# A selective-scan stage on one Trainium2 core: dt's product leaves PSUM by Relu, the second half's x projection is done in one go from DRAM, the gate of y comes a slot later, and dt's sum is on GpSimd

## The chip, the cores and the metric

The kernel runs on one core of one Trainium2 chip. The metric is device time in microseconds of one execution. Engines are called PE (TensorE), DVE (VectorE), ACT (ScalarE), POOL (GpSimd) and SP (SyncE, which here only issues transfers). All data are fp32; a few matmul operands are read in the fp32r format. The core has on-chip memory of 128 partitions (SBUF), and PSUM with eight banks of 128 x 512 fp32, into which PE writes.

## The reference

Eight layers run one after the other on an activation of 2 x 1024 x 1024, each with a residual and a layer norm: attention, grouped feed-forward, convolution with block attention, a binary-weight product, a selective scan, an int4 product, attention, and a product with routed low-rank terms. Only the selective scan (the reference's `_L2_attn_ref`) is touched:

```python
proj = hidden_states @ in_proj_w                      # 1024 -> 2 x 2048
x, z = split(proj)
xc = silu(conv_b + causal 4-tap convolution of x)     # per channel, along time
ssm_p = einsum('bdl,ed->ble', xc, x_proj_w)           # 2048 -> 64 + 16 + 16
dt_r, Bm, Cm = rmsnorm of the three parts of ssm_p
dt = softplus(dt_r @ dt_proj_w.T + dt_bias)           # 2048 channels
A = -exp(A_log)                                       # 2048 x 16
h = exp(dt * A) * h + dt * B * x                      # step by step in time, 16 states per channel
y = (sum over the states of h * C + D * xc) * silu(z)
out = y @ out_proj_w.T
```

The kernel writes softplus(p) as max(p, 0) + ln(1 + e) + (e - ((1 + e) - 1)) with e = exp(-|p|); the last bracket gives back what is lost when 1 + e is rounded.

## The kernel before, in words

The program treats the two batch elements one after the other, and everything in this section happens twice. In the scan layer a batch element has 1024 time steps, taken as two halves of 512 (`u` = 0, 1), and 2048 channels, taken as 16 chunks of 128 (`c`).

**What comes before the scans.** `l2_in` (L999) computes the first half: for each chunk a product of eight matmuls into a PSUM bank, a copy with the convolution's first tap on ACT (`l2_x`), three taps on DVE (`l2_taps`, L985), Silu on ACT, a write of the result to DRAM (`xcd`, L991), and the x projection (`l2_px`, L997), which accumulates over the chunks in one PSUM bank. `l2_norm` and `l2_spread` turn that bank into dt_r, B and C.

**The slots.** The scan is a loop over slots `k`, with its order written out by hand (a manual schedule: each engine receives its instructions in the order of the text). A chunk of one half takes 8 slots, 128 slots make a half, 256 both. A slot handles 2 x 128 rows, each row a (state, channel) pair with 512 time steps:

- SP loads `h` (L1117, 128 rows x 2 x 512): dt times x of the slot's channels, read from DRAM (`dxd`) so that 16 partitions get the same row. It is issued six slots ahead; there are nine buffers.
- POOL multiplies `h` by B, two slots ahead (`times_b`, L1123).
- PE spreads dt over the states (`decay`, L1130), and ACT takes the exponent in place in PSUM (L1132), one slot ahead, twice a slot.
- DVE runs two scans (L1137), and multiplies the slot before by C (`times_c`, L1148).
- PE sums the states into the bank `py` of the chunk (`states`, L1159), every second slot.

**Work on a chunk's edge.** Work for later slots is put down with `at(slot, f)`; it runs in the middle of its slot, behind the first scan, the first decay and its exponent, and ahead of the second scan. For each chunk `l2_dt` (L1055) starts 16 slots before the chunk's own scans: the product p on PE (L1060) in the first slot, and then one step per slot, in this order:

```python
for n, f in enumerate((act1, act2, pool1, sum1, parts, low)):
    at(k + 1 + n, f)
at(k + 8, load)
```

`act1` takes Abs of p and Exp (L1071, L1072), `act2` 1 + e and Ln (L1075, L1076), `pool1` three operations on POOL (L1079 to L1081), `sum1` adds max(p, 0) on DVE straight out of PSUM (L1084), `parts` copies dt to `hi` on ACT (L1087) and multiplies it by x on POOL (L1088, x comes in as `xi`, whose load is issued at slot k + 3), and writes the product to `dxd` (L1090), `low` makes the low part on POOL (L1093) and writes `hi` and `lo` to DRAM (L1095); `load` reads them back (L1100). The tiles `e`, `one`, `lg`, `hi` and `lo` have one buffer each.

At the end of a chunk `y_out` (L1175) multiplies the bank `py` by silu(z) on DVE (L1177) and writes it to DRAM. Its operand `zs` (one buffer) is loaded by `y_in` at slot 4 of each eight, and `y_out` is put down five slots later, in the same slot as the last `states` of that chunk.

**Work beside the scans.** PE has other matmuls to do in the meantime; they stand in a list, `todo`, and each slot takes the next 17 of every 8 slots in the first half, 14 of 8 in the second: the gates of the first half (128 matmuls), the x of the second half (`ins(1)`, 128 matmuls, each chunk followed by taps, Silu and x projection through `at`), the gates of the second half (128), and from slot 140 on the out product of the first half (`outs(0)`). The loads of the weights stand in a queue of their own, `ahead`, in order, each with the number of calls by which it goes ahead.

**Buffers.** All PSUM tiles share one pool of eight banks. `self.w()` gives one of eight buffers of 128 x 1024, of which two hold dt's weights through the layer. SP takes its transfers in the order of the text, and waits at one that isn't ready.

Of the kernel before, what the change touches and what calls it, by code (L numbers as in the profile page):

```python
# [8 lines left out]
F = mybir.dt.float32  # L9
I = mybir.dt.int32  # L10
R = mybir.dt.float32r
AF = mybir.ActivationFunctionType
ALU = mybir.AluOpType
# [4 lines left out]
P = 128  # L18
# [9 lines left out]
class Net:  # L28
# [892 lines left out]
    def l2_attn(self, b):  # L921
# [4 lines left out]
        with (  # L926
# [4 lines left out]
            cw = self.param(lp, "l2_convw", [P, NCH, 4])  # L931
            cb = self.param(lp, "l2_convb", [P, NCH])
            dpar = self.param(lp, "l2_D", [P, NCH])
            A = self.param(lp, "l2_Alog", [P, NCH * N])
            nc.scalar.activation(A, A, AF.Exp)
            nc.vector.tensor_scalar(A, A, -1.0, None, ALU.mult)
# [34 lines left out]
            def at(k, f, *args):  # L971
                late.setdefault(k, []).append((f, args))
# [21 lines left out]
            def l2_px(u, c, acc):  # L994
                if c == 0:
                    px[u] = self.ps()
                nc.tensor.matmul(  # L997
                    px[u][:NF, :], wx[:, c * NF : (c + 1) * NF], acc, start=c == 0, stop=c == NCH - 1
                )  # L999
# [57 lines left out]
            def l2_dt(u, c, k):  # L1057

                p = self.ps()
                nc.tensor.matmul(  # L1060
                    p, wd[c // 8][: NF + 1, (c % 8) * P : (c % 8 + 1) * P], norms[u][0], start=True, stop=True
                )
                xs[u, c] = xc = tmp("xi")
                at(k + 3, nc.sync.dma_start, xc, xcd[u][c][:])
                e, one, lg = tmp("e", 1), tmp("one", 1), tmp("lg", 1)
                dt, dtx = lg, e
                hi = tp.tile([P, HALF], R, tag="hi", bufs=1, name=self.nm("hi"))
                lo = tp.tile([P, HALF], R, tag="lo", bufs=1, name=self.nm("lo"))

                def act1():  # L1070
                    nc.scalar.activation(e, p, AF.Abs)  # L1071
                    nc.scalar.activation(e, e, AF.Exp, scale=-1.0)  # L1072

                def act2():
                    nc.scalar.activation(one, e, AF.Identity, bias=self.one)  # L1075
                    nc.scalar.activation(lg, one, AF.Ln)  # L1076

                def pool1():
                    nc.gpsimd.tensor_scalar(one, one, 1.0, None, ALU.subtract)  # L1079
                    nc.gpsimd.tensor_tensor(e, e, one, ALU.subtract)  # L1080
                    nc.gpsimd.tensor_tensor(lg, lg, e, ALU.add)  # L1081

                def sum1():
                    nc.vector.scalar_tensor_tensor(dt, p, 0.0, lg, ALU.max, ALU.add)  # L1084

                def parts():
                    nc.scalar.copy(hi, dt)  # L1087
                    nc.gpsimd.tensor_tensor(dtx, dt, xc, ALU.mult)  # L1088
                    for j in range(4):
                        nc.sync.dma_start(dxd[u][c][:, j, :], dtx[32 * j : 32 * j + 32, :])  # L1090

                def low():
                    nc.gpsimd.tensor_tensor(lo, dt, hi.bitcast(F), ALU.subtract)  # L1093
                    for s, t in ((0, hi), (1, lo)):
                        nc.sync.dma_start(hld[u][c][:, s, :], t.bitcast(F))  # L1095

                def load():
                    t = qp.tile([P, 2, HALF], F, tag="hl", bufs=2, name=self.nm("hl"))
                    for s in range(2):
                        nc.sync.dma_start(  # L1100
                            t[64 * s : 64 * s + 64], hld[u][c][:, s, :].rearrange("(a r) t -> r a t", a=2)
                        )
                    hl[u, c] = t
# [4 lines that stand above are left out]
# [72 lines left out]
            def ins(u):  # L1180

                def one(u, c):
                    u0 = u * HALF
                    w = {}

                    def load():
                        w["w"] = self.w(i["l2_in"][c])

                    def call(k, now):
                        if k == 0:  # L1190
                            w["p"] = self.ps()
                        p = w["p"]
                        nc.tensor.matmul(  # L1193
                            p, w["w"][:, k * P : (k + 1) * P], self.xcols(k, u0, HALF), start=k == 0, stop=k == KD - 1
                        )
                        if k == KD - 1:
                            def x():
                                w["x"] = l2_x(u, c, p)
                            at(now + 1, x)
                            at(now + 2, lambda: l2_taps(c, p, w["x"]))  # L1200

                            def s():
                                w["s"] = l2_silu(u, c, p)
                                self.table()
                            at(now + 3, s)
                            at(now + 5, lambda: l2_px(u, c, w["s"]))
                            if c == NCH - 1:
                                at(now + 6, lambda: at(now + 8, l2_spread, u, l2_norm(u)))
                    return load, [(call, k) for k in range(KD)]
                return [one(u, c) for c in range(NCH)]  # L1210

            def gates(u):

# [70 lines left out]
            with self.tc.manual_schedule():  # L1284

                todo, ahead = [], []

                def take(units, lead):
                    for n, (load, calls) in enumerate(units):
                        ahead.append((len(todo) - lead, load))  # L1290
                        todo.extend(calls)

                take(gates(0), 20)
                take(ins(1), 20)
                take(gates(1), 20)
                taken = 0
                at(-BEFORE, lambda: at(4 - BEFORE, l2_spread, 0, l2_norm(0)))
                for k in range(-BEFORE, 2 * SL + 6):
                    if -16 <= k < 2 * SL - 16 and k % 8 == 0:
                        l2_dt((k + 16) // SL, (k + 16) % SL // 8, k)  # L1300
                    if k == SL + 12:
                        take(outs(0), 8)
                    if k == -1 or k == SL:
                        l2_cr(max(k, 0) // SL)
                    n = 3 if k < -1 else 2 + (k % 8 == 0) if k < SL else 2 - (k % 4 == 3)
                    batch = []
                    for _ in range(n):
                        while ahead and ahead[0][0] <= taken:
                            ahead.pop(0)[1]()
                        if taken < len(todo):  # L1310
                            batch.append(todo[taken])
                            taken += 1

                    def pe(last=False):
                        while batch and (last or len(batch) > n - 1):
                            f, *args = batch.pop(0)
                            if f:
                                f(*args, k)

                    live = 0 <= k < 2 * SL  # L1320
                    if 0 <= k + 6 < 2 * SL:
                        rows(k + 6)
                    if 0 <= k + 2 < 2 * SL:
                        times_b(k + 2)
                    if 0 <= k - 1 < 2 * SL:
                        keep(k - 1)
                    pe()
                    for m in range(2):
                        if live:
                            scan(k, m)  # L1330
                        if 0 <= k + 1 < 2 * SL:
                            decay(k + 1, m)
                        if m:
                            break
                        if k % 2 == 1 and 0 <= k - 2 < 2 * SL:
                            states(k - 2)
                        for f, args in late.pop(k, []):
                            f(*args)
                        pe(True)
                    if 0 <= k - 1 < 2 * SL:  # L1340
                        times_c(k - 1)
                    if live and k % 8 == 4:
                        v = y_in(k)
                        at(k + 5, lambda k=k, v=v: y_out(k, v))
                    if live and k % 8 == 0:
                        skip(k // SL, k % SL // 8)
                while late:
                    for f, args in late.pop(min(late)):
                        f(*args)
# [439 lines left out]
```

## Time and profile before

| | |
|---|---|
| Time, median of 3 runs | 5673.8 us (5659.03 to 5676.83) |
| Profiled execution, its own time | 5686.25 us |
| Its span | 5684.5 us |
| Busy share of the span: PE, DVE, POOL, ACT | 88%, 57%, 36%, 33% |
| Mean granted TensorE clock | 0.934 |
| Slots 0 to 255 of the first batch element | 1174.7 to about 2236 us |
| Slots 0 to 255 of the second | 4014.7 to about 5060 us |
| One scan (L1137), `times_c` (L1148), on DVE | 1.21 to 1.27, 1.195 us |
| `times_b` (L1123), on POOL | 2.37 us |
| One exponent (L1132), on ACT | 0.66 us |
| dt's sum (L1084) and y's gate (L1177), on DVE | 0.67 and 0.69 us |
| POOL with a scalar (L1079), POOL with two tensors (L1080, L1081, L1088, L1093), 128 x 512 | 1.49, 1.27 us |

The busy share is a mean over eight layers with different limits; the scans take about 2107 of 5684 us. "Idle before" an instruction is the time its engine stood still ahead of it, put down to what ended it. A wait of SP holds back all transfers behind it. The share of the DMA engines counts the time in which they have packets in work, and the rate in GB/s what they moved.

### The profile page before, as it was taken

To read this page: it belongs to the slowest core of one execution; us is meant where nothing else is said; L and a number is where in the kernel's file an instruction comes from. 1 tells how busy PE (TensorE), PEld (TensorE's weight loads), DVE (VectorE), ACT (ScalarE), POOL (GpSimd) and SP (SyncE) were. 2 spreads that over 40 slices of the span, in tenths; PEclk is the share of its full clock that TensorE was granted. 3 is DMA by queue.
4 is the path that set the end of the run, shared out by engine and by line. 5 is a ranking of instruction groups with operands and counts; after the bars stand their busy time and mean duration, and the time that the engine had idled before them with its cause. 6 is when DMAs were issued, how large, how long until landed. Compare 5 with 4: busy or idle time off the path is not lost.

```text
span 5684.5 us, 50188 instructions
## 1 busy us (share of the span) xinstructions
PE 5023.3 (88%) x16840; PEld 2396.8 (42%) x16840; DVE 3258.3 (57%) x4474; ACT 1858.8 (33%) x3795; POOL 2033.7 (36%) x1193
## 2 busy tenths in 40 slices
PE   9879979998888887998989799899988887889989
PEld 4346646433333222454444376464333332234533
DVE  3553245269889897214345412452798999962243
ACT  2320232266656442001013311323666564420010
POOL 1031120077678774100010211200776787741000
PEclk8889988999999998999988899889999999989999
DMA  2135301298789997201110333012987899961100
GB/s 90 41 126 178 100 32 43 97 242 236 214 224 270 253 261 209 81 30 41 48 67 30 115 123 99 30 42 100 251 231 217 232 267 261 270 196 61 60 8 30
DMA packets 295094, 782.85 MB, mean 138 GB/s; under 512 B 40976, under 2 KB 58000, under 8 KB 294836
## 3 DMA queue, kind: packets, MB, share of 16 engines
q1 hardware_dynamic: 288564, 758.66, 46.8%
q0 software_dynamic: 6272, 20.98, 1.1%
q8 instruction: 135, 2.21, 0.2%
q14 instruction: 123, 1.01, 0.1%
HBM read 640.81 MB, written 136.58 MB: 137 GB/s over the span
## 4 chain that ended last, share of the span: by engine, by line
PE 43%; DVE 13%; DMA 8%; ACT 3%; issue 3%; POOL 2%; SPq 0%; DVEq 0%; POOLq 0%; ACTq 0%
PE ps L104 21%; DVE h L1137 5%; PE ps L1436 4%; PE ps L579 3%; PE ps L1226 3%; DVE h L1148 3%; PE ps L1159 2%; DMA xi<-xcd 2%; DMA h<-dxd 2%; PE ps L120 2%; POOL h L1123 1%; ACT ps L1132 1%; PE ps L1130 1%; DMA w<-yd 1%; DVE x L165 1%
## 5 line engine op out<-in xcount | busy, mean ns | idle before, releaser
L1123 POOL TENSOR_TENSOR h<-h,br 128x1024 f32<-128x1024 f32 x512 | 1199.2, 2366 | 67.6 <-DMA h<-dxd 38.8
L1132 ACT ACTIVATE ps<-ps,l_Alog 128x512 f32<-128x512 f32 x1024 | 666.8, 659 | 844.9 <-PE ps L1130 818.7
L1130 PE MATMUL ps<-hl,rep 128*128 128x512 f32 x1024 | 706.1, 701 | 137.4 <-DVE h L1137 106.3
L1137 DVE TENSOR_TENSOR_SCAN h<-ps,h 128x512 f32<-128x512 f32 x512 | 608.7, 1211 | 68.6 <-ACT ps L1132 65.8
L1137 DVE TENSOR_TENSOR_SCAN h<-ps,hst,h 128x512 f32<-128x512 f32 x512 | 635.4, 1269 | 19.8 <-POOL h L1123 18.5
L1148 DVE TENSOR_TENSOR h<-h,ps 128x1024 f32<-128x1024 f32 x512 | 611.4, 1195 | 0.0
L1159 PE MATMUL ps<-h,sel 128*32 128x512 f32 x2048 | 462.1, 656 | 131.0 <-DVE h L1148 128.9
L104 PE MATMUL ps<-w,xT 128*128 128x512 f32 (+1 forms) x1280 | 515.6, 560 | 0.0
L1226 PE MATMUL ps<-xT,w 128*128 128x512 f32 x1024 | 515.2, 607 | 0.1
L1130 PEld LDWEIGHTS ps<-hl,rep 128*128 128x128 f32 x1024 | 201.2, 199 | 563.6 <-DVE h L1137 325.6
L131 DVE TENSOR_TENSOR x<-x,ps 128x512 f32<-128x512 f32 x192 | 129.3, 683 | 519.2 <-PE ps L104 369.6
L1422 POOL TENSOR_TENSOR x<-x,row 128x1024 f32<-128x1024 f32 x48 | 113.2, 2361 | 876.3 <-PE ps L120 876.3
L104 PE MATMUL ps<-xT,w 128*128 128x512 f32 x960 | 425.1, 599 | 0.2 <-DMA w<-l_wqkv 0.2
L104 PEld LDWEIGHTS ps<-w,xT 128*128 128x128 f32 x1280 | 246.5, 194 | 253.5 <-issue 246.6
L120 PE MATMUL ps<-ident,x 128*128 128x128 f32 x1024 | 166.0, 318 | 180.7 <-DVE x L165 153.4
L1079 POOL TENSOR_SCALAR one<-one 128x512 f32<-128x512 f32 x64 | 95.5, 1493 | 575.1 <-ACT lg L1076 544.2
L1226 PEld LDWEIGHTS ps<-xT,w 128*128 128x128 f32 x1024 | 188.6, 191 | 223.0 <-issue 202.2
L104 PEld LDWEIGHTS ps<-xT,w 128*128 128x128 f32 x960 | 183.9, 192 | 233.3 <-issue 232.5
L1193 PE MATMUL ps<-xT,w 128*128 128x512 f32 x512 | 275.9, 626 | 2.8 <-DVE h L1137 2.8
L1265 PE MATMUL ps<-w,w 128*128 128x512 f32 x512 | 275.0, 619 | 2.2 <-DVE h L1137 2.2
L156 ACT ACTIVATE rs<-mv 128x1 f32<-128x1 f32 (+2 forms) x94 | 19.1, 203 | 780.5 <-DVE mv L150 780.2
L985 DVE SCALAR_TENSOR_TENSOR ps<-xp,l_convw,ps 128x512 f32<-128x512 f32 x192 | 144.5, 753 | 199.0 <-ACT ps L980 194.4
(262 smaller groups left out, 7234.0 us busy)
## 6 DMA issues: line engine op xcount, KB each, us to landing
h<-dxd SPq DMA_DIRECT2D x512, 512.0 KB
w<-l_in SPq DMA_DIRECT2D x128, 512.0 KB
w<-l_out SPq DMA_DIRECT2D x96, 512.0 KB
hl<-hld SPq DMA_DIRECT2D x128, 256.0 KB
w<-l_conv SPq DMA_DIRECT2D x54, 512.0 KB
w<-cvd SPq DMA_DIRECT2D x36, 512.0 KB
w<-l_fw SPq DMA_DIRECT2D x32, 512.0 KB
xcd<-xo SPq DMA_DIRECT2D x64, 256.0 KB
```

What stands on the lines that cost most here:

```text
L104: self.nc.tensor.matmul(out, lhsT, rhs, start=j == 0, stop=j == n - 1)
L120: nc.tensor.transpose(p[:, j * P : (j + 1) * P], self.x[:, tt, k * P : (k + 1) * P], self.ident)
L1123: nc.gpsimd.tensor_tensor(hs[k], hs[k], norms[of(k)[0]][1].unsqueeze(1).to_broadcast([P, 2, HALF]), ALU.mult)
L1130: nc.tensor.matmul(dA[k, m], rep[:, 4 * m + q, :], hl[u, c][:, jj, :].bitcast(R), start=True, stop=True)
L1132: nc.scalar.activation(dA[k, m], dA[k, m], AF.Exp, scale=A[:, g : g + 1])
L1137: nc.vector.tensor_tensor_scan(hs[k][:, m, :], dA.pop((k, m)), hs[k][:, m, :], hst[:, g : g + 1] if u else 0.0, ALU.mult, ALU.add)
L1148: nc.vector.tensor_tensor(hs[k], hs[k], norms[of(k)[0]][3].unsqueeze(1).to_broadcast([P, 2, HALF]), ALU.mult)
L1159: nc.tensor.matmul(py[u, c][32 * j : 32 * j + 32, :], self.sel[:, q, :], hs[k - 1 + j // 2][:, j % 2, :], start=False, stop=q == 3,)
L1193: nc.tensor.matmul(p, w["w"][:, k * P : (k + 1) * P], self.xcols(k, u0, HALF), start=k == 0, stop=k == KD - 1)
L1226: nc.tensor.matmul(p, w["w"][:, k * P : (k + 1) * P], self.xcols(k, u * HALF, HALF), start=k == 0, stop=k == KD - 1)
L1265: nc.tensor.matmul(p, y[:, cc, t * P : (t + 1) * P], wt[:, cc * HALF : (cc + 1) * HALF], start=c2 == 0 and cc == 0, stop=last,)
L1436: nc.tensor.matmul(acc[tt], y[:, cc * HALF + tt * P : cc * HALF + (tt + 1) * P], w[:, cc * HALF : (cc + 1) * HALF], start=c == 0, stop=c = ...
```

## The change

- **dt's product leaves PSUM by Relu.** `act1` first writes max(p, 0) to `hi` on ACT. `sum1` is no longer a DVE operation on PSUM, but an addition on POOL of two tiles in SBUF. The bank of p is free after `act1` (slot k + 1), where it was held to `sum1` (slot k + 4).
- **(1 + e) - 1** is a third operation of `act2` on ACT, with a tile of -1 as its bias; it was POOL's operation with a scalar.
- **x projection of the second half.** `ins(1)` no longer calls `l2_px`, `l2_norm` and `l2_spread`. New units, `xproj(1)`, stand in the list of matmuls behind the first two units of the gates of the second half: eight units, each of two transfers of 256 KB from `xcd` into one `w` buffer, and two calls. Their loads go four calls ahead (those of the gates twenty), and the loads of the later gates stand behind them in `ahead`.
- **The gate of y** is put down six slots after `y_in`, where it was five.

```diff
+            neg = lp.tile([P, 1], F, name=self.nm("neg"))
+            nc.gpsimd.memset(neg, -1.0)
...
                 def act1():
+                    nc.scalar.activation(hi.bitcast(F), p, AF.Relu)
                     nc.scalar.activation(e, p, AF.Abs)
                     nc.scalar.activation(e, e, AF.Exp, scale=-1.0)
 
                 def act2():
                     nc.scalar.activation(one, e, AF.Identity, bias=self.one)
                     nc.scalar.activation(lg, one, AF.Ln)
+                    nc.scalar.activation(one, one, AF.Identity, bias=neg)
 
                 def pool1():
-                    nc.gpsimd.tensor_scalar(one, one, 1.0, None, ALU.subtract)
                     nc.gpsimd.tensor_tensor(e, e, one, ALU.subtract)
                     nc.gpsimd.tensor_tensor(lg, lg, e, ALU.add)
 
                 def sum1():
-                    nc.vector.scalar_tensor_tensor(dt, p, 0.0, lg, ALU.max, ALU.add)
+                    nc.gpsimd.tensor_tensor(dt, lg, hi.bitcast(F), ALU.add)
...
-                            at(now + 5, lambda: l2_px(u, c, w["s"]))
-                            if c == NCH - 1:
-                                at(now + 6, lambda: at(now + 8, l2_spread, u, l2_norm(u)))
...
+            def xproj(u):
+
+                def one(c2):
+                    w = {}
+
+                    def load():
+                        w["x"] = self.w()
+                        for n in range(2):
+                            nc.sync.dma_start(w["x"][:, n * HALF : (n + 1) * HALF], xcd[u][2 * c2 + n][:])
+
+                    def call(n, now):
+                        l2_px(u, 2 * c2 + n, w["x"][:, n * HALF : (n + 1) * HALF])
+                        if 2 * c2 + n == NCH - 1:
+                            at(now + 1, lambda: at(now + 3, l2_spread, u, l2_norm(u)))
+                    return load, [(call, n) for n in range(2)]
+                return [one(c2) for c2 in range(NCH // 2)]
...
-                take(gates(1), 20)
+                z1 = gates(1)
+                take(z1[:2], 20)
+                take(xproj(1), 4)
+                take(z1[2:], 20)
...
-                        at(k + 5, lambda k=k, v=v: y_out(k, v))
+                        at(k + 6, lambda k=k, v=v: y_out(k, v))
```

## The prediction, made before the result was known

> **What bounds the kernel now.** The change touches the scan layer alone, so I read stages first: the busy time by stretch (first batch element; slots 0 to 32, 32 to 88, 88 to 112, 112 to 160, 160 to 256). Columns: PE, PE weight loads, DVE, ACT, POOL busy, PE clock, DMA share, GB/s.
>
> ```profile
> 1174.70:1296.00 121.30, 113.33 (x341) 43.89 (x340) 111.78 (x103) 80.98 (x150) 97.65 (x52) 1.00 0.99 256
> 1296.00:1554.90 258.90, 218.43 (x630) 79.37 (x630) 231.42 (x228) 169.43 (x313) 183.95 (x96) 0.94 0.84 224
> 1554.90:1668.60 113.70, 90.86 (x272) 34.83 (x271) 99.52 (x103) 60.84 (x119) 72.81 (x39) 0.91 0.80 213
> 1668.60:1844.00 175.40, 158.44 (x484) 59.24 (x484) 173.10 (x157) 109.91 (x183) 151.99 (x80) 0.98 1.01 267
> 1844.00:2236.00 392.00, 306.76 (x870) 105.47 (x869) 359.95 (x330) 154.34 (x252) 281.09 (x143) 0.90 0.95 249
> ```
>
> DVE is busiest everywhere, but its idle differs: 9.5, 27.5, 14.2, 2.3 and 32.0 us. The transfers differ too: the first, fourth and fifth stretches move 249 to 267 GB/s, near the fastest stretch I found (275), and only the second and third have room. The waits of DVE say what each idle is. Slots 32 to 88:
>
> ```profile
> DVE zs L1177 <- PE ps L1159: 13.4, 7, 3.4
> DVE h L1137 <- ACT ps L1132: 11.6, 9, 3.0
> ```
>
> Half of it is y's gate standing in front of the state sums of its own slot, half a scan whose exponent is late. Slots 160 to 256:
>
> ```profile
> DVE lg L1084 <- POOL lg L1081: 14.5, 6, 4.5
> DVE h L1137 <- POOL h L1123: 12.5, 5, 4.2
> DVE zs L1177 <- PE ps L1159: 4.5, 6, 0.8
> ```
>
> Here POOL is late, and POOL's own waits in that stretch give the cause, x's transfer:
>
> ```profile
> POOL e L1088 <- DMA xi<-xcd: 47.1, 8, 8.3
> POOL h L1123 <- DMA h<-dxd: 13.7, 13, 2.4
> ```
>
> Last, the timeline of SP and ACT around a chunk's edge in that stretch, for the new use of `hi`:
>
> ```profile
> 2080.36 0.53 SPq L1095 DMA_DIRECT2D hld<-hi  x1
> ...
> 2082.66 0.59 ACT L1071 ACTIVATE e<-ps 128x512 f32<-128x512 f32 x1
> ...
> 2086.79 0.59 SPq L1100 DMA_DIRECT2D hl<-hld  x1
> ```
>
> SP issues L1100 when `hi` has landed in DRAM: 4.1 us after the next chunk's Abs began.
>
> **What the Trainium skill says.** "ScalarE: Activation LUTs", section on table sets: relu, copy, identity and abs are in every set, so Relu and Identity bring no table load; the trace agrees for Abs and Identity between Exp and Ln (a load would show as 1.28 us). "SBUF — State Buffer", section on its two sides: GpSimd and a DVE operation with two SBUF inputs exclude each other for a whole instruction. The scans and the product with C take one operand from PSUM, and keep their 1.21 and 1.195 us under a busy POOL; the norm's tiny DVE operations do not (L1027 took 2.40 us, a POOL product 2.37). So POOL's new addition doesn't slow the scans. "Perfetto Trace Analysis", optimization strategy: a gap that repeats can mean that no PSUM buffer was free. The trace agrees: PE's decays wait for DVE's scans, 106 us before the matmul and 326 before its weights.
>
> **The change, part by part.** Per batch element, against the profiled execution; 32 chunks, 0.67 us per dt sum.
>
> *DVE loses the sum:* 32 x 0.67 = 21.4 us of work, worth something only where DVE sets the pace. *POOL* trades 1.49 for 1.27 us. *ACT* gains a Relu (0.59, as Abs from PSUM) and an Identity (0.72): 1.3 us per chunk, on an engine busy 65% in the first half; the exponents queued behind them have 0 to 4 us before their scans.
>
> *PSUM:* p's bank comes free three slots earlier, and the x projection no longer holds a bank from about slot 32 to 94; y's holds one for a slot more. From the built programs I counted, for each decay, how many scans back lies the one that freed its bank. In slots 32 to 96 of the old program 30 of 128 decays take the bank of the scan just ahead (two back in half-slots), 68 three back; in the new one none take two back, 41 three, 66 four. The late exponents of slots 32 to 96 should mostly go.
>
> *Gate a slot later:* the state sums it waits for are then one slot (3.6 us or more) old; the longest wait was 3.4. It removes nearly all 13.4 us in slots 32 to 88. Its write is issued only two slots before SP wants `zs` again; now it is 8 to 15 us before, and the chain shows writes of 9.2. SP may stand 1 to 2 us there per chunk; the next load of `h` must wait for a slot's end anyway, except where SP is already late (slots 160 on).
>
> *x projection:* 16 matmul pairs leave the taps' stretch, and stand in slots 96 to 104 instead, with 16 transfers of 256 KB (4.2 MB). Per slot there: `h` 0.52 MB, x 0.56, the rest 0.26, together 1.34 MB; at 268 GB/s 5.0 us against 3.7 to 4.1 now. Loads go four calls (two slots) ahead, and PE stands in order before them, with the decays behind: 8 slots x 1.2 = 10 us. The norm's stall of some 18 us (8 slots of 50.6 instead of 33) moves from slot 93 to 105. The later gates' weights, queued behind, are called six matmuls after their issue.
>
> *The wait that the change adds:* Relu writes `hi`, whose last reader is the write to DRAM. ACT would wait from Abs's start to the landing. Taking this difference for every chunk gives waits in 3 chunks of slots 0 to 40 (0.8, 2.8, 3.5) and 9 of the late ones (0.4 to 5.7): 39 us of ACT. Shifting the following exponents by it, and subtracting what each had before its scan, leaves 16 us late at DVE (0 to 4.9 each); some lies where POOL makes DVE late anyway.
>
> The sum, by stretch:
> - slots 0 to 32: 4 x 0.67 of work and 3.7 of waits (6.4), less 2.5 for Relu, and transfers at 0.99: **1** gained
> - 32 to 88: 7 x 0.67 = 4.7, and 15.7 of the 26 us of waits (60%, since PE at 84% busy keeps some): **20**
> - 88 to 112: now 113.7; then 31 for the first eight slots (29.1 as where DVE never idles, 0.67 less, one set of taps 2.3), 42 for the next (8 x 5.0, and 2 for the weights behind), 46.5 with the norm (28.5 + 18), together 119.5: **-6**
> - 112 to 160: 6 x 0.67 = 4, halved for transfers at 267 GB/s: **2**
> - 160 to 256: 12 x 0.67 = 8 and 14.5 of waits, less 13 for Relu, 2 for SP at `zs`, and half the rest, since transfers set the pace: **4**
>
> 21 us, for two batch elements 42: the profiled execution goes from 5686 to 5644. The median is 12.5 us below it: **5632**.
>
> **Rivals.**
> - *The wait on `hi` takes all back (slower).* All 39 us of ACT's waits fall on DVE, with 32 x 0.59 of Relu in front of exponents: 58 us per element, against 36 gained without the wait (21 + 15). It decides from 36 us on; at its worst 5674 + 2 x 22 = 5718. For it: the chunks where it falls are DVE's tight ones. Against it: 2 to 4 us lie between most exponents and their scans there, and banks free earlier give more.
> - *Transfers set everything but slots 32 to 88 (no change).* 4.2 MB at 268 GB/s is 15.7 us; the second stretch gives 20, the others nothing: 4 us per element, 5665. For it: DMA shares of 0.95 to 1.01. Against it: 213 GB/s in the third stretch.
> - *Everything is recovered (much faster).* Second stretch 26 + 4.7, first 6, fourth 4, fifth 30, x projection -3: 68 per element, 5538. For it: the late stretch's idle hangs on a loop of dt sum, load of x, product; against it: 249 GB/s there.
> - *The change doesn't do what it says:* the gate waits for PE a slot later too, if PE is a slot behind. It costs 10 per element; 5652.
>
> **How the numbers follow.** Forecast 0.48 (own range 5605 to 5660), recovered more 0.14, transfers 0.18, gate 0.06, `hi` 0.14. A change within 0.3% (17 us) can't be told from none. Faster: 0.44 + 0.14 + 0.06 + 0.03 = 0.67 with half of the gate's; I take 0.65. Same: 0.04 + 0.10 + 0.03 + 0.02 = 0.19. Slower: the rest of transfers and `hi`, 0.16. The range leaves out the outer halves of the recovered and the `hi` case: 5575 to 5695.
>
> **What would show it.** DVE's wait of L1177 on PE falls from 49 us to under 10. The scans' wait for ACT falls in slots 32 to 88. Slots 96 to 104 take about 40 us, with PE waiting for w <- xcd. ACT waits for hld <- hi some 20 to 40 us per element, mostly past slot 160. DVE's wait on POOL at the sum is gone, and the wait of POOL for xi stays. Wrong: if slots 160 to 256 take over 395 us, the new wait or SP's stand at `zs` sets their pace; if under 370, transfers didn't.

## The result, and the profile after

The changed kernel takes 5588.7 us (median of 4 runs, 5577.0 to 5606.4) against 5669.3 us (4 runs, 5659.0 to 5676.8): ratio 0.986, 95% interval 0.983 to 0.989, so 80 us or 1.4% faster, where 42 us were forecast. The time lies in the range, the direction was right, and the gain was nearly twice the forecast. The profiled execution of before (5686 us) is one of the slower ones, that of after (5577 us) the fastest: between the two traces lie 109 us, of which 105 fall in the scans. Sums over stretches below are therefore some 30% above the gain of the medians.

The busy time by stretch, first batch element of the kernel after, in the same slots as in the prediction (columns again PE, PE weight loads, DVE, ACT, POOL, clock, DMA share, GB/s):

```profile
1171.30:1289.20 117.90, 112.73 (x341) 43.98 (x340) 109.08 (x98) 84.98 (x158) 98.46 (x53) 1.00 0.99 267
1289.20:1522.90 233.70, 206.77 (x604) 77.82 (x603) 226.20 (x222) 176.17 (x328) 180.58 (x94) 0.96 0.89 247
1522.90:1624.20 101.30, 86.77 (x270) 32.27 (x269) 88.91 (x100) 59.45 (x119) 67.03 (x38) 0.98 0.91 249
1624.20:1800.60 176.40, 162.48 (x492) 61.03 (x490) 169.85 (x151) 117.81 (x196) 157.83 (x83) 0.98 0.98 272
1800.60:2170.70 370.10, 306.81 (x892) 107.67 (x891) 349.68 (x316) 171.41 (x277) 276.39 (x142) 0.94 1.00 269
```

Three stretches moved. Slots 32 to 88 went from 258.9 to 233.7 us, with DVE idle for 7.5 us where it was idle for 27.5. Slots 88 to 112, which were to get longer, went from 113.7 to 101.3. Slots 160 to 256 went from about 391 to 370, at 269 GB/s instead of 249. The waits of DVE in slots 32 to 88:

```profile
DVE h L1140 <- ACT ps L1135: 5.4, 8, 1.7
DVE ps L987 <- ACT ps L982: 0.9, 2, 0.7
```

The gate's wait for the state sums (13.4 us there) is gone, and the scans' wait for exponents is down from 11.6 to 5.4. Waits of ACT in slots 160 to 256, with the new one:

```profile
ACT ps L1135 <- PE ps L1133: 154.2, 134, 7.5
ACT hi L1073 <- DMA hld<-hi: 30.6, 7, 7.7
ACT hi L1090 <- POOL lg L1087: 7.3, 6, 1.7
```

The wait for the write of `hi` is there: 30.6 us here, 38.9 us in the whole first element, 37.8 in the second. The prediction had worked out 39. It also reaches DVE, whose waits in the same stretch are:

```profile
DVE h L1140 <- ACT ps L1135: 11.5, 4, 5.6
DVE h L1140 <- POOL h L1126: 8.7, 5, 2.8
```

Before, DVE waited 0.3 us for exponents here; now it waits 11.5 us (10.6 in the second element).

The x projection's new place, slots 96 to 104 and 104 to 112, in the first and then in the second element:

```profile
1552.60:1587.70 35.10, 25.94 (x84) 8.58 (x83) 28.15 (x27) 19.02 (x35) 19.95 (x12) 1.00 1.05 276
1587.70:1624.20 36.50, 32.92 (x102) 12.87 (x101) 31.13 (x47) 19.59 (x42) 24.12 (x14) 0.95 0.87 248
4330.10:4361.10 31.00, 25.43 (x84) 8.71 (x82) 27.64 (x26) 19.02 (x35) 20.33 (x13) 1.00 1.05 309
4361.10:4400.60 39.50, 31.94 (x99) 12.64 (x98) 35.18 (x47) 19.38 (x41) 24.70 (x14) 0.91 0.84 229
```

All kernels below are read by one table: the time from the start of the first scan of one stretch to that of the next, mean of the two batch elements, in us. A stretch that an edit does not touch differs by 1 to 4 us from kernel to kernel, slots 160 to 256 by up to 10 between the two elements of the kernel before (390.5 and 379.9). Each row is one execution, which need not be a typical one of its kernel; what an edit is worth to the whole is read from the times.

| | 0-32 | 32-88 | 88-112 | 112-160 | 160-256 | sum |
|---|---|---|---|---|---|---|
| before | 119.5 | 257.4 | 113.5 | 175.4 | 385.2 | 1051.0 |
| after | 117.4 | 233.1 | 101.5 | 176.5 | 370.1 | 998.5 |
| e1 gate only | 118.1 | 251.5 | 111.3 | 177.0 | 382.3 | 1040.0 |
| e2 dt only | 117.8 | 246.3 | 109.2 | 173.1 | 370.8 | 1017.2 |
| e3 x projection only | 118.7 | 238.1 | 107.7 | 177.1 | 371.9 | 1013.4 |
| e4 after, Relu later | 117.7 | 230.3 | 100.9 | 175.1 | 368.9 | 992.9 |
| e5 e3 with the bank held | 119.4 | 255.9 | 110.5 | 177.6 | 376.8 | 1040.2 |
| e6 16 empty calls | 118.8 | 256.5 | 106.9 | 176.7 | 373.7 | 1032.6 |
| e7 before, norm in PSUM | 120.6 | 258.0 | 104.4 | 175.4 | 385.7 | 1044.0 |
| e8 after, norm in PSUM | 117.9 | 233.0 | 103.1 | 175.9 | 371.6 | 1001.3 |
| e9 8 empty calls | 121.1 | 256.2 | 105.8 | 175.0 | 380.3 | 1038.4 |
| e10 32 empty calls | 118.2 | 257.1 | 106.3 | 176.3 | 373.2 | 1031.0 |
| e11 after, gate back | 119.1 | 234.7 | 104.7 | 174.8 | 373.2 | 1006.3 |
| e12 after, Relu later, loads earlier | 117.8 | 232.1 | 106.2 | 175.6 | 369.1 | 1000.6 |

### The profile page after: what moved, and what is told of

Same layout as the page of the kernel before. It is cut to its first block, busy times and chain, and to the rows that moved or that the text cites. A ratio compares the mean times of both kernels' runs of the same rounds, so it can differ in the third digit from the quotient of the medians.

```text
span 5575.3 us, 50352 instructions
## 1 busy us (share of the span) xinstructions
PE 5005.2 (90%) x16840; PEld 2400.9 (43%) x16840; DVE 3201.0 (57%) x4410; ACT 1933.0 (35%) x3923; POOL 2017.6 (36%) x1195
## 4 chain that ended last, share of the span: by engine, by line
PE 57%; DVE 15%; DMA 13%; ACT 5%; issue 3%; POOL 1%; SPq 1%; DVEq 0%; POOLq 0%; ACTq 0%
PE ps L104 28%; PE ps L579 5%; DVE h L1140 5%; PE ps L1243 4%; PE ps L1456 4%; DVE h L1151 3%; PE ps L1162 2%; DMA xi<-xcd 2%; DMA h<-dxd 2%; PE ps L120 2%; DMA hl<-hld 2%; ACT ps L1135 2%; PE ps L1133 1%; DMA w<-yd 1%; DMA hld<-hi 1%
## 5 line engine op out<-in xcount | busy, mean ns | idle before, releaser
L1133 PE MATMUL ps<-hl,rep 128*128 128x512 f32 x1024 | 745.9, 735 | 79.9 <-DVE h L1140 69.1
L1162 PE MATMUL ps<-h,sel 128*32 128x512 f32 x2048 | 497.4, 635 | 133.3 <-DVE h L1151 128.4
L1442 POOL TENSOR_TENSOR x<-x,row 128x1024 f32<-128x1024 f32 x48 | 113.3, 2362 | 877.1 <-PE ps L120 877.1
L1083 POOL TENSOR_TENSOR e<-e,one 128x512 f32<-128x512 f32 x64 | 81.7, 1276 | 535.3 <-ACT one L1080 466.0
L1162 PEld LDWEIGHTS ps<-h,sel 128*32 128x32 f32 x2048 | 69.9, 109 | 448.6 <-DVE h L1151 315.3
```

What stands on the lines that cost most here:

```text
L1133: nc.tensor.matmul(dA[k, m], rep[:, 4 * m + q, :], hl[u, c][:, jj, :].bitcast(R), start=True, stop=True)
L1162: nc.tensor.matmul(py[u, c][32 * j : 32 * j + 32, :], self.sel[:, q, :], hs[k - 1 + j // 2][:, j % 2, :], start=False, stop=q == 3,)
```

## The experiments

The theory from this profile: the parts overlap, and what the prediction got wrong is the price of the wait on `hi`, the x projection's stretch, and the last stretch. The rival: one part alone carries the gain.

### Each part alone, and the wait on `hi` taken away

**e1, the gate alone.**

```diff
-                        at(k + 5, lambda k=k, v=v: y_out(k, v))
+                        at(k + 6, lambda k=k, v=v: y_out(k, v))
```

> The kernel before, with the gate of y alone put down a slot later. If the gate's wait for the state sums was a loss of its own, DVE's 47 us of waits at this line in the two scan stages (26.1 and 21.4) go, mostly in slots 32 to 112, and the time falls by 25 to 45 us. If the wait only stood in for the exponents that are late anyway (no PSUM bank free), the scans' wait for ACT grows by about the same, and the time falls by less than 10 us.

Measured: 5658.0 us, ratio 0.997 (0.996 to 0.999): 15 us by the ratio, 18 by the medians. Between the two expectations, nearer the second. DVE's waits in slots 32 to 88 of this kernel:

```profile
DVE h L1137 <- ACT ps L1132: 17.4, 11, 2.7
DVE lg L1084 <- POOL lg L1081: 0.5, 2, 0.3
```

The gate's 13.4 us are gone, and the exponents' wait has grown from 11.6 to 17.4. The stretch gains 6 us, not 13. The bank of y is held a slot longer here, so that more decays must take the bank of the scan just ahead, counted in the order of the program; that this is why the exponents wait longer fits e5 below, and no run isolates it.

**e2, dt alone:** the first two points of the change, edited as in the diff of the change.

```diff
+                    nc.scalar.activation(hi.bitcast(F), p, AF.Relu)
...
+                    nc.scalar.activation(one, one, AF.Identity, bias=neg)
...
-                    nc.gpsimd.tensor_scalar(one, one, 1.0, None, ALU.subtract)
...
-                    nc.vector.scalar_tensor_tensor(dt, p, 0.0, lg, ALU.max, ALU.add)
+                    nc.gpsimd.tensor_tensor(dt, lg, hi.bitcast(F), ALU.add)
```

> The kernel before, with dt's product out of PSUM by Relu, (1+e)-1 on ACT and dt's sum on GpSimd alone. If DVE's work sets the pace, 64 x 0.67 = 43 us of it go, and 28 us of DVE's waits for POOL at the sum, and the bank of p is free three slots earlier: 30 to 50 us faster. If transfers set the pace past slot 160, and ACT's new wait for the write of hi falls on the scans, 0 to 15 us faster; ACT waits for hld <- hi 30 us or more per batch element.

Measured: 5615.9 us, ratio 0.990 (0.988 to 0.991): 60 us, above the first expectation's upper end. 11 us per element come from slots 32 to 88, 14 from slots 160 to 256, though ACT waits 33 us for `hld <- hi` in the first element.

**e3, the x projection alone:** `xproj` as in the diff of the change, and

```diff
-                            at(now + 5, lambda: l2_px(u, c, w["s"]))
...
-                take(gates(1), 20)
+                z1 = gates(1)
+                take(z1[:2], 20)
+                take(xproj(1), 4)
+                take(z1[2:], 20)
```

> The kernel before, with the x projection of the second half alone done in one go. As the prediction had it (transfers at 268 GB/s, 5.0 us per slot in slots 96 to 104, the norm's stall only moved), 0 to 15 us slower. If instead the PSUM bank and the matmuls that it takes out of slots 32 to 88 count, and the transfers of slots 96 to 104 go at 280 GB/s or more, 15 to 35 us faster.

Measured: 5621.6 us, ratio 0.990 (0.988 to 0.992): 55 us. The prediction's term had the wrong sign, and the rival's range was too low as well. 19 us per element come from slots 32 to 88, 6 from 88 to 112, 13 from 160 to 256, where no x projection is. The three parts give 15, 60 and 55 us alone, 130 in sum, and 80 together: they are in part substitutes for each other.

**e4, the Relu later.**

```diff
                 def act1():
-                    nc.scalar.activation(hi.bitcast(F), p, AF.Relu)
...
+                def relu():
+                    nc.scalar.activation(hi.bitcast(F), p, AF.Relu)
...
+                at(k + 3, relu)
                 at(k + 8, load)
```

> The kernel after, with the Relu two slots later (slot k + 3 of its chunk): it no longer meets the write of hi of the chunk before, and p's bank is held two slots longer. If ACT's wait for that write (30.6 us past slot 160 of the first batch element, and the like in the second) delays the scans, it goes from 39 us per element to under 5, and the time falls by 10 to 25 us. If the exponents have enough room before their scans, or transfers set the pace there, the wait goes and the time stays within 8 us; if the bank is what counts, slots 32 to 88 get slower by 5 us or more.

Measured: 5591.5 us, ratio 0.986 (0.984 to 0.987), that of the kernel after. ACT's waits in slots 160 to 256 of the first element:

```profile
ACT ps L1138 <- PE ps L1136: 164.1, 135, 7.5
ACT hi L1092 <- POOL lg L1089: 24.9, 8, 7.1
ACT e L1073 <- DMA dxd<-e: 1.9, 3, 1.4
```

The wait for `hld <- hi` is gone entirely, and ACT now stands instead before the copy of dt, for POOL's sum (24.9 us, in the kernel after 7.3). DVE's waits in this stretch:

```profile
DVE h L1143 <- POOL h L1129: 18.5, 6, 5.6
DVE h L1143 <- ACT ps L1138: 1.4, 1, 1.4
```

DVE's wait for exponents is gone (11.5 to 1.4 us), and its wait for POOL's products has grown by the same amount (8.7 to 18.5); in the second element it is 10.6 to 0 and 9.5 to 18.4. DVE stands idle for about 20 us either way, and the stretch keeps its length, 368.9 against 370.1. So the wait on `hi` did reach DVE, but taking it away brought nothing: the time that DVE no longer waits for ACT it waits for POOL. POOL's own waits for loads of `h` grew with it, from 13.9 to 23.2 us in the first element, which fits the transfers as what holds the stretch. The slots 32 to 88 did not suffer from the bank held longer (230.3 against 233.1).

### What the x projection gained: the bank, and the shift

**e5, the bank held.** On top of e3, the first of the 16 products stays at its old place, so that the accumulation's bank is taken through slots 32 to 96 as before; the other 15 stay away.

```diff
                             at(now + 3, s)
+                            if c == 0:
+                                at(now + 5, lambda: l2_px(u, c, w["s"]))
...
-                        l2_px(u, 2 * c2 + n, w["x"][:, n * HALF : (n + 1) * HALF])
+                        if c2 or n:
+                            l2_px(u, 2 * c2 + n, w["x"][:, n * HALF : (n + 1) * HALF])
```

> The kernel of the x projection alone, but with the first of its 16 products left at its old place (slot 37 or so), so that its accumulation holds one PSUM bank through slots 32 to 96, as before the change; the other 15 products stay out of the taps' stretch. In the built program the decays take the banks of the same scans as before the change (15 of 64 the one just ahead). If the bank made the x projection's gain in slots 32 to 88 (257 to 238 us, mean of both elements), they go back to 250 us or more. If the 15 pairs of matmuls that left PE made it, they stay at 238 to 242 us. Slots 160 to 256 aren't touched: 372 us either way.

Measured: 5663.4 us, ratio 0.998 (0.997 to 0.998): of the 55 us, 12 are left. Slots 32 to 88 of both elements, first with the bank free (e3), then with it held (e5):

```profile
1297.70:1535.70 238.00, 203.46 (x601) 76.47 (x600) 230.86 (x229) 168.38 (x313) 183.00 (x96) 0.95 0.90 243
4092.20:4330.30 238.10, 204.90 (x601) 77.63 (x600) 230.78 (x229) 168.79 (x314) 179.63 (x94) 0.94 0.88 238
```

```profile
1300.80:1556.20 255.40, 209.90 (x604) 74.95 (x603) 231.25 (x228) 168.94 (x313) 183.21 (x95) 0.93 0.82 226
4125.30:4381.60 256.30, 208.64 (x605) 74.15 (x605) 231.12 (x229) 168.99 (x313) 183.29 (x96) 0.95 0.81 225
```

DVE has the same 231 us of work, and the stretch is 238 or 256 us long by one bank alone. This separates the two explanations: the gain of the x projection in this stretch (19 us) is the bank, not the 15 matmul pairs that left PE. DVE's waits in the first element, with the bank free (e3) and with it held (e5):

```profile
DVE zs L1177 <- PE ps L1159: 3.6, 4, 2.1
DVE h L1137 <- ACT ps L1132: 1.7, 4, 0.6
```

```profile
DVE zs L1177 <- PE ps L1159: 12.1, 7, 2.6
DVE h L1137 <- ACT ps L1132: 9.9, 9, 2.3
```

The gate stands in its old slot in both, so most of its wait too went with the bank. The clock doesn't explain it: 0.95 and 0.94 with the bank free, 0.93 and 0.95 with it held.

**e6, only shifted.** The kernel before, with 16 empty calls where the x projection would stand, so that the later gates and the out product come 9 slots later.

```diff
-                take(gates(1), 20)
+                z1 = gates(1)
+                take(z1[:2], 20)
+                take([(lambda: None, [(None,)] * 16)], 4)
+                take(z1[2:], 20)
```

> The kernel before, with 16 empty calls in the list of matmuls where the x projection stands after the change: the later gates and the out product come as many calls (9 slots) later, and nothing else changes. If slots 160 to 256 got faster with the x projection alone (385 to 372 us) because the out product's loads now fall otherwise among the slots, they fall to 370 to 377 us here too. If the freed bank or the state of the queues did it, they stay at 380 us or more. Slots 32 to 88 stay at 257 us.

Measured: 5660.2 us, ratio 0.998 (0.996 to 0.999). Slots 160 to 256 of both elements:

```profile
1837.30:2213.80 376.50, 307.30 (x890) 105.99 (x889) 356.48 (x326) 159.76 (x257) 278.68 (x142) 0.93 0.99 263
4653.30:5024.30 371.00, 306.08 (x886) 106.71 (x886) 356.13 (x326) 159.94 (x257) 278.72 (x142) 0.94 0.99 267
```

They fall to 373.7, nearly as with the x projection: the shift is enough by itself in this stretch, and neither the bank nor POOL's sum is needed for it. It is not the only way, since e2, which shifts nothing, gets to 370.8. The rate is up to 263 and 267 GB/s. The granted clock is 0.93 and 0.94 here, and 0.90 and 0.91 in this stretch before; a higher clock is not needed, since the second element of e2 took 372.7 us at 0.90. The table overstates the shift: the times give 15 us for both elements and all stretches together, under 8 per element, where the row gives 11.5 for this stretch alone.

Slots 88 to 112 are shorter here too, by 6.6 us. About half of that lies in slots 96 to 112, in the first eight of which the empty calls stand in place of matmuls. The rest is in slots 88 to 96 of the second element (43.4 us, in the first 50.4), and belongs to the norm's small operations, which come up under e7.

**e9 and e10, other shifts.** The same with 8 and with 32 empty calls, one profiled run each.

```diff
-                take([(lambda: None, [(None,)] * 16)], 4)
+                take([(lambda: None, [(None,)] * 8)], 4)
```

> The kernel before, with 8 empty calls instead of 16: gates and out product come 4 to 5 slots later. Slots 160 to 256 take 385 us before (mean of two elements) and 374 with 16 calls. If later is better (fewer loads compete ahead of slot 160's backlog), they take 377 to 383. If it is the place of the out product's loads among the eight slots of a chunk, 8 calls are another place, and the time can lie on either side: 365 to 392.

> The kernel before, with 32 empty calls: gates and out product come some 18 slots later. If later is better, slots 160 to 256 take less than the 374 us of 16 calls, 355 to 368, since part of the out product falls behind the last scan. If it is the place among the slots, they take 370 to 390 with no order by length.

Measured: 5660.4 and 5660.9 us; slots 160 to 256 take 380.3 and 373.2 us. In these traces eight calls give under half of what 16 give, and 32 no more than 16, so that later is not always better. With one trace each, and up to 10 us between two elements of one execution, the order of 8 and 16 is not firm, and the times of e6, e9 and e10 (5660.2 to 5660.9 us) don't differ. All kernels that got this stretch down, by whichever part, end at 369 to 377 us, at 261 to 272 GB/s with a DMA share of 0.96 to 1.01: it looks like a floor that the transfers set, which the kernel before missed by 10 to 20 us. Which meeting of loads made it miss it was not isolated.

### The norm in the x projection's stretch

**e7, the norm's small tiles in PSUM, in the kernel before.** Its sums of squares and the factor of the root's correction lie in unused columns of a PSUM tile, so that every small DVE operation has an operand there; a Square on ACT takes the place of one product.

```diff
-                ss = self.small([P, 4, 3], "ss")
+                q = p[:, 4 * NF :].rearrange("p (n t j) -> p n t j", t=4, j=4)
+                ss, rt = q[:, 0, :, :3], q[:, 1, :, :3]
...
-                self.rsqrt(rr, ss)
+                rr, ry, r2 = (self.small([P, 4, 3], t) for t in ("rr", "ss", "rsq"))
+                self.table()
+                nc.scalar.activation(ry, ss, AF.Ln)
+                nc.scalar.activation(ry, ry, AF.Exp, scale=-0.5)
+                nc.scalar.activation(r2, ry, AF.Square)
+                nc.vector.tensor_tensor(rt, r2, ss, ALU.mult)
+                nc.vector.tensor_scalar(rt, rt, -0.5, 1.5, ALU.mult, ALU.add)
+                nc.vector.tensor_tensor(rr, ry, rt, ALU.mult)
```

> The kernel before, with the norm's small tiles in PSUM, so that none of its seven small DVE operations reads SBUF alone or from two tiles of SBUF (one small Square more on ACT). If the 2.3 us of four of them (L1027, L160, L161, L162) are GpSimd's product holding the ports, each takes under 0.4 us, slots 88 to 112 fall from 113.5 to about 105 us, and the time by 12 to 20 us. If it is the latency of the chain through ACT, they stay within 3 us.

Measured: 5665.3 us, ratio 0.998 (0.998 to 0.999): 10 us, a little under the expected 12. Slots 88 to 112 fall to 104.4 in both elements, 9.1 us less. Groups of DVE around the norm, in the kernel before and then in e7:

```profile
L1027 DVE TENSOR_SCALAR ss<-ss 128x8 f32<-128x8 f32 x1 | 2.4, 2403 | 0.0
L161 DVE TENSOR_SCALAR rsq<-rsq 128x12 f32<-128x12 f32 x1 | 2.3, 2267 | 0.0
L160 DVE TENSOR_TENSOR rsq<-rsq,ss 128x12 f32<-128x12 f32 x1 | 2.3, 2266 | 0.0
L162 DVE TENSOR_TENSOR rr<-rr,rsq 128x12 f32<-128x12 f32 x1 | 2.3, 2260 | 0.0
```

```profile
L1035 DVE TENSOR_SCALAR ps<-ps 128x12 f32<-128x12 f32 x1 | 0.2, 177 | 0.0
L1034 DVE TENSOR_TENSOR ps<-rsq,ps 128x12 f32<-128x12 f32 x1 | 0.2, 176 | 0.7 <-ACT rsq L1033 0.7
L1028 DVE TENSOR_SCALAR ps<-ps 128x8 f32<-128x8 f32 x1 | 0.2, 174 | 0.0
```

These four operations on 8 or 12 elements took 2.3 us each with all operands in SBUF, and they take 0.18 us with an operand in PSUM. Half of the norm's stall was DVE standing behind GpSimd's products, as "SBUF — State Buffer" of the Trainium skill (section on the two sides of SBUF) describes it. The page names DVE operations with two SBUF inputs or in a mode that uses both ports; L1027 and L161 read one tile only, and were held like the other two. It does not happen each time: in the second element of e6 L1027, L160 and L162 stand unchanged in SBUF and take 0.16 to 0.17 us (L159 1.7, L161 0.3).

**e8, the same edit in the kernel after.**

> The kernel after, with the norm's small tiles in PSUM in the same way. The change's profile had the small operations free of GpSimd's product in the first element and two of them behind it in the second. If that is chance of place, slots 104 to 112 fall in the second element from 39.5 to about 36 us, in the first they stay, and the time stays within 10 us of the kernel after (0 to 8 us faster).

Measured: 5591.7 us, ratio 0.985 (0.982 to 0.987), as the kernel after. Slots 104 to 112 fall from 39.5 to 37.2 us in the second element, and from 36.5 to 35.7 in the first. The change had lost most of that stall by itself. In the kernel after DVE runs the same operations in SBUF in 0.17 us each, and POOL's timeline says why:

```profile
1590.82 2.36 POOL L1126 TENSOR_TENSOR h<-h,br 128x1024 f32<-128x1024 f32 x1 [0.93 <-DMA h<-dxd]
1595.03 4.67 POOL L1126 TENSOR_TENSOR h<-h,br 128x1024 f32<-128x1024 f32 x2 [1.84 <-DMA h<-dxd]
```

POOL stands idle from 1593.2 to 1595.0, waiting for a load of `h`, and the five small operations from L1029 to the end of the root (1593.1 to 1594.6) fall into that gap. In the second element two of them still take 2.3 and 1.7 us. It is a chance of place: POOL was late at the right moment. The x projection is not needed for such a chance: in the second element of e6, which does the x projection at its old place, three of the operations fell between products of POOL.

### Two variants of the kernel after

**e11, the gate back.**

```diff
-                        at(k + 6, lambda k=k, v=v: y_out(k, v))
+                        at(k + 5, lambda k=k, v=v: y_out(k, v))
```

> The kernel after, with the gate of y put back to five slots after its load; all else stays. If the gate's wait is a loss of its own, DVE waits there again for 20 us or more per element and slots 32 to 112 take 8 to 14 us more: 20 to 35 us slower than the kernel after. If the gate brings as little as alone (15 us of 5676), 5 to 17 us slower.

Measured: 5588.8 us, ratio 0.983 (0.980 to 0.987) against before, so no slower than the kernel after. Its trace has 9.1 and 14.0 us of waits at the gate, and a sum of stretches 8 us longer, which the times do not show. Both expectations were too high: in the kernel after the gate's slot is worth nothing that these runs can tell.

**e12, Relu later and the x projection's loads eight calls ahead.**

```diff
-                take(xproj(1), 4)
+                take(xproj(1), 8)
```

> The kernel after, with the Relu two slots later and the x projection's loads eight calls ahead instead of four. PE waited 26 us for these loads in the first element (16.6 before weights, 9.2 before matmuls). If they hold the slots 96 to 104 up, these go from 35 and 31 us to 29 to 31, and the time falls by 5 to 12 us under the kernel after. If the transfers themselves are the limit there (276 to 309 GB/s), it stays within 4 us.

Measured: 5593.6 us, ratio 0.986 (0.982 to 0.990). PE's wait for these loads in the first element falls from 26 us to 4, and slots 96 to 104 take 38.1 and 33.4 us, more than before the edit. So their lead does not hold these slots. The loads of dt's x come late in their place (POOL waits 9.7 us for one), and the rate is 279 and 316 GB/s at a share of 1.04: that fits transfers that hold the slots, though the order of the loads changed too. No variant beats the kernel after.

## Why the prediction was right or wrong

The step that failed most is the term for the x projection in slots 88 to 112, which had the wrong sign: it put a loss of 6 us per element where 12 were gained. The second is the term for slots 160 to 256, which was far too small: 4 us where 15 were gained. The mechanisms of slots 32 to 88 were right. By the prediction's own sum, per batch element, from the traces (mean of the two elements):

- **Slots 32 to 88, forecast 20 gained, measured 24.3.** Right in mechanism and nearly in size, but not in the split. Banks and the gate were named; nearly all of the gate's 13.4 us was put down to its slot, where e5 shows that the bank is the larger part, and e1 (6 us in this stretch) and e11 (nothing in its time) that the slot is the smaller. The 60% of the waits was too careful: DVE is idle for 7.5 of 233.7 us now, and three edits that would give 6, 11 and 19 alone meet at this floor.
- **Slots 88 to 112, forecast 6 lost, measured 12.0 gained.** Off by 18 us per element, in two figures of about the same weight. The first is 42 us for slots 96 to 104; they took 35.1 and 31.1 us. Rate times length gives 9.7 and 9.6 MB moved, and not the 10.7 of the prediction (8 x 1.34), which at its own 268 GB/s would be 36 us: an estimate from these figures is that 6 of the 9 us were too many bytes and the 2 us added for weights. Only ten of the 16 loads of x are issued in these slots, the others before, and six loads of `h` instead of eight. The other 3 us are the rate, 276 and 309 GB/s, where the rates of whole stretches had been taken as a ceiling. What made the rate is not shown. The second figure, 18 us for the norm that is only moved: 9 of them were the small operations held behind GpSimd (e7), which depends on what POOL does just then. The prediction named this, with its 2.40 us for one tiny operation, and still carried the stall over as a fixed cost. Slots 104 to 112 took 36.5 and 39.5, not 46.5.
- **Slots 160 to 256, forecast 4 gained, measured 15.1.** Two faults. The wait on `hi` was found and sized rightly (39 us of ACT forecast; 38.9 and 37.8 measured), and so was its share at DVE (13 us forecast here; DVE's wait for exponents grew to 11.5 and 10.6). But it was subtracted as a loss on top of all else, and e4 shows that it overlaps with another: without it DVE waits as much longer for POOL, and the stretch keeps its length. That DVE there only follows the transfers fits the rate, and is not shown. And the shift of the out product by 16 calls was put at nothing, without a reason, though by its trace it brings 11.5 us alone (e6), by the times less. The prediction's list of what moves had the transfers added by the x projection, and not that everything behind them in the list comes nine slots later. The gains do not add: dt alone (14.4), the x projection alone (13.3) and the shift alone each reach nearly the same length.
- **Slots 112 to 160 and 0 to 32, forecast 2 and 1 gained, measured 1 lost and 2 gained.** Within what one trace tells.

So the sum had 21 per element, and the traces have 52.5, the medians 40. The signs shown by the profile were mostly as forecast: DVE's wait at the gate fell from 49.0 to 1.3 us, PE waits for w <- xcd, ACT waits for hld <- hi within the range given, and the wait of DVE for POOL at the sum is gone. "Slots 96 to 104 take about 40 us" was wrong, and "DVE is busiest everywhere" was a misreading of the first stretch, where PE is busy for 113.3 us and DVE for 111.8. Slots 160 to 256 ended at 370.1 us, just at the 370 under which transfers were not to set the pace. The rival in which `hi` takes all back is refuted by the gain and by e4, that in which transfers leave only slots 32 to 88 by the other two stretches; the one in which the gate goes on waiting by its 1.3 us. The gain lies about halfway between the forecast and "everything recovered" (68 per element), which had a chance of 0.14.

What stays open: which loads meet in slots 160 to 256 of the kernel before, so that a shift shortens them, and how much of it holds beyond single traces.

## What to carry to other kernels

A PSUM bank that an accumulation holds over a long stretch is missing to all who rotate through the rest; moving the accumulation away was worth 19 us per element by the bank alone here, even at the price of reading its operands again from DRAM. A wait that a change adds is not a loss on top of the waits that are there: here 10 us of DVE's idle time only changed the engine that it waited for. Ask first what holds the stretch, and charge the wait to that. An edit that puts work into a shared list also moves everything behind it, and that move is a part of its own, to be costed like the others.

## What the runs showed of the hardware that was not expected

- Four DVE operations of 8 to 12 elements took 2.26 to 2.40 us each behind GpSimd's products of 2.37 us, and 0.16 to 0.18 us with an operand in PSUM or in a gap of GpSimd's. In the kernel after and in e6 which of the two occurs changed from one element to the next within one execution.
- The highest transfer rates over eight slots, 309 GB/s (316 in e12), came in slots 96 to 104 of the second element, with the plain loads of 256 KB for the x projection; slots 160 to 256, where about half of the bytes are loads of `h` that put one row on 16 partitions, stopped at 261 to 272 GB/s with a share of about 1.0. Eight slots of the kernel before without the x projection's loads reached 276 (slots 104 to 112), so the kind of load is not shown to be the cause.
- GpSimd's operation with a scalar on 128 x 512 took 1.49 us, more than its operation on two tensors (1.27 us).
